# Layer 3 of a four-layer graph network: VectorE's second joined block and the preceding unit's reciprocals change places

## The chip, the cores and the metric

The program runs on one core of a Trainium2 chip, in one launch. The metric is the device time of a launch in microseconds (us). The core has five engines with queues of their own: TensorE (PE; its weight loads are listed apart as PEld), VectorE (DVE), ScalarE (ACT), GpSimd (POOL) and SyncE (SP), which here only issues DMA transfers. An engine works through its queue in the order in which the program was written, and waits where an input or a buffer is not there yet.

## The reference

`x` is 32 x 512 x 64 (32 batches, 512 nodes, 64 features) and `adj` a normalised 512 x 512 adjacency matrix. Four layers follow each other, each with a layer norm before it and a residual around it; layers 0 to 2 are a plain graph layer, a two-step propagation and a small attention. The change is in layer 3, graph attention with 8 heads of width 128 and an output layer of the same form:

```
def gat_layer(x, graph, W, b):
    h = x @ W
    s = jnp.einsum('bnd,bmd->bnm', h, h) * graph
    s = jnp.where(s == 0.0, NEG_INF, s)
    a = jax.nn.softmax(s, axis=2)
    return jnp.einsum('bnm,bmd->bnd', a, h) + b
heads = jax.vmap(lambda W, b: gat_layer(flow_x, graph, W, b))(Wh, bh)
...
x = jax.nn.leaky_relu(cat, negative_slope=0.01)
out = gat_layer(x, graph, W_out, b_out)
return jax.nn.leaky_relu(out, negative_slope=0.01)
```

## The kernel before

Everything is float32. Layers 0 to 2 run first (to about 460 us of the span); layer 3 takes the rest. It is cut into **units**: a unit is two attention maps of 512 x 512 that are worked on together (`k` = 0, 1), held as four row blocks `r` = 0 to 3 of 128 partitions x 1024 elements. For each two batches there are eight units of heads (`Heads`) and one of the output layer (`Out`), which comes some units later; 16 pairs of batches make 144 units.

A unit goes through these steps (line numbers are those of the profile):

- `scores(r)`, PE, L370: row block `r` of the scores into a PSUM tile of pool `ps_s`.
- `maxima(r)`, DVE, L382: masks the block, copies it negated to SBUF (`p_att`), and takes row maxima into `top`. Two instructions a block.
- `spread_out`, L389 and L392: DVE transposes the maxima (`top_t`), SP sends them to DRAM (`top_row`, four small transfers). `spread_in`, L398: SP reads them back, spread over all partitions (`topb`, 512 KB).
- `shift(r)`, POOL, L404: subtracts `topb` from block `r`.
- `exps(r)`, ACT, L413: the exponential. For `r` = 0 and 2 it stays in SBUF; for `r` = 1 and 3 it goes to a PSUM tile `e_ps` of the same pool `ps_s`.
- `join(r)`, DVE, L416, `r` = 1 and 3: adds the exponentials of blocks `r` - 1 and `r`. The result is the joined block, and `e_ps` comes free.
- `totals`, PE L434, ACT L439: column sums of joined blocks 1 and 3 with a matmul of ones. `totals_out`, L446: SP and ACT send them to a small tile `parts`, 8 to a partition.
- `recips`, DVE, L452 and L455: adds the two sums and takes reciprocals (`rec_flow`, 128 x 8). `recips_out`, SP, L459: to DRAM (`rec_row`). `recips_in`, SP, L466: back from there, spread over 64 partitions for each map (`recb`, two transfers of 128 KB).
- `values(j)`, PE, L422: the blocks times the features, into `av` (pool `ps_v`, one buffer). `normalize`, DVE, L472: `av` times `recb` gives `o_att` and frees `av`.
- `y_pe`, `y_act`, `y_dve` (L553, L563, L571): the head's product with its weights, bias and leaky ReLU. `back`, `back_dve`, `back_pool`, `store`: the end of an output unit.

`ps_s` has two buffers (line 1260), and they are taken in turn by blocks 2 and 3 of the scores, blocks 0 and 1 of the next unit's scores, and the two `e_ps`, all in one period. So block 2 of the next period's scores needs what `join(1)` frees, and block 3 what `join(3)` frees.

The order is written by hand. `planned` (L703) makes a function `period(t)` (L711), which is called for `t` = -10 onward and writes one period: the steps of units of different age next to each other. `unit(1)` is the unit one period old, `unit(2)` two periods, and so on; a step that a unit hasn't got does nothing. The schedule is kept as written for all five engines, so VectorE's queue in a period is: `maxima` 2 and 3 of the present unit, the transpose of `top`, `y_dve` of unit(4), `normalize` of unit(3), `maxima` 0 and 1 of the coming unit, `join(1)` of unit(1), `recips` of unit(2), `back_dve`, `join(3)` of unit(1), and now and then a small reduction (`features`, `judge_product`, or the difference in `make_v`). SP's queue is: `recb` of unit(3), `top_row`, `topb`, one `parts`, `rec_row`, and the stores of an output unit.

```
def join(self, r):
    nc.vector.tensor_tensor(self.p[r], self.joined, self.p[r - 1], OP.add)
...
def recips(self):
    self.rec = tiny.tile([P, 8], F32, name="rec_flow")
    nc.vector.tensor_reduce(
        self.rec, self.parts.rearrange("p e i -> p i e"), AX.X, OP.add
    )
    nc.vector.reciprocal(self.rec, self.rec)
...
def normalize(self):
    self.o = wk.tile([P, N], F32, name="o_att")
    nc.vector.tensor_tensor(self.o, self.av, self.recb, OP.mult)
```

Of the kernel before, what the change touches and what calls it, by code (L numbers as in the profile page):

```python
# [22 lines left out]
def fast_form(  # L23
# [645 lines left out]
    def any_zero():  # L669

        def across(src, rows, name):
            ps = ps_m.tile([P, P], F32, name=name, tag="m")
            n = src.shape[0]
            nc.tensor.transpose(ps[:rows, :n], src, ident[:n, :n])
            return ps[:rows, :n]

        own = tiny.tile([P, 1], F32, name="own")
        nc.vector.tensor_reduce(own, least, AX.X, OP.min)
        two = tiny.tile([1, 2], F32, name="two")
        nc.vector.tensor_reduce(two[:, 0:1], across(own, 1, "own_ps"), AX.X, OP.min)  # L680
        best = tiny.tile([B // 2, 2], F32, name="best")
        nc.vector.tensor_reduce(
            best,
            across(least_out, B // 2, "out_ps").rearrange("b (k f) -> b k f", k=2),
            AX.X, OP.max,
        )
        worst = tiny.tile([B // 2, 1], F32, name="worst")
        nc.vector.tensor_reduce(worst, best, AX.X, OP.min)
        nc.vector.tensor_reduce(
            two[:, 1:2], across(worst, 1, "worst_ps"), AX.X, OP.min  # L690
        )
        flag = tiny.tile([1, 1], F32, name="flag")
        nc.vector.tensor_reduce(flag, two, AX.X, OP.min)
        nc.vector.scalar_tensor_tensor(
            again, flag, 0.0, unsound, op0=OP.is_equal, op1=OP.max
        )
# [6 lines left out]
    def planned(units, products):  # L703

        class Nothing:
            def __getattr__(self, name):
                return lambda *args: None

        nothing = Nothing()

        def period(t):  # L711
            def unit(lag):
                return units[t - lag] if 0 <= t - lag < len(units) else nothing

            now, ahead = unit(0), unit(-1)
            for r in range(2, C):
                now.scores(r)
            unit(3).recips_in()
            unit(4).y_pe()
            unit(1).shift(0)  # L720
            unit(1).exps(0)
            unit(4).y_act()
            u, h = products.get(t - 1, (None, 0))
            if u and h == H - 1:
                u.keep_product()
            unit(1).shift(2)
            unit(1).exps(2)
            for r in range(2, C):
                now.maxima(r)
            now.spread_out()  # L730
            now.spread_in()
            for r in range(2):
                ahead.scores(r)
            unit(4).y_dve()
            unit(3).normalize()
            for r in range(2):
                ahead.maxima(r)
            unit(4).back()
            unit(2).totals()
            unit(2).totals_out()  # L740
            unit(1).shift(1)
            unit(1).exps(1)
            u, h = products.get(t, (None, 0))
            if u:
                u.product(h)
            for j in range(C):
                unit(2).values(j)
            unit(1).join(1)
            unit(1).shift(3)
            unit(1).exps(3)  # L750
            unit(5).back_pool()
            unit(-2).make_gs()
            unit(2).recips()
            unit(2).recips_out()
            unit(5).store()
            unit(4).back_dve()
            unit(1).join(3)
            unit(-3).features(3)
            unit(-2).judge_product()
            unit(1).make_v()  # L760
            unit(-4).make_hx()
            unit(-2).make_g()
            for step in range(3):
                for lag, odd in ((step - 7, 0), (step - 11, 1)):
                    u = unit(lag)
                    if getattr(u, "i", None) == 0 and u.b % 2 == odd:
                        u.features(step)
            if t == len(units):
                any_zero()

        return period
# [1067 lines left out]
```

## Time and profile before

| | |
|---|---|
| median of 3 runs | 2102.34 us (2097.67 to 2103.63) |
| profiled execution, time / span | 2099.58 us / 2097.8 us |
| mean granted TensorE clock | 0.985 |
| layer 3, first to last transpose of `top` (L389) | 460.7 to 2053.4 us, 144 of them |
| busy in that stretch of 1592.7 us: PE, DVE, POOL, ACT | 1542.6, 1404.6, 1379.1, 1029.0 us |

The stretch of 1592.7 us divided by its 143 periods gives 11.14 us for a period. Four engines are busy in it, none of them all the time: what one unit needs is spread over six periods, and the engines hand its parts to each other. So busy shares alone don't say what sets the period; the waits and the order within one period do. A row of a timeline gives the start, the duration, the engine, the line and operation, and in brackets how long the engine had been idle and what ended that.

### The profile page before, as it was taken

What the parts mean: (1) busy time and instruction counts of PE and PEld (TensorE: products, weight loads), DVE (VectorE), ACT (ScalarE), POOL (GpSimd) and SP (SyncE); (2) the same over time, 40 slices, a digit from 0 to 9 for tenths busy, and PEclk for the clock granted to TensorE, in tenths of its full rate; (3) what the DMA queues carried; (4) which work ended last, traced back from release to release, by engine and by line L of the source; (5) the groups of instructions that cost most, each with busy time, mean ns of one, the idle gap of its engine ahead of it and who ended that gap; (6) DMA issues with size and microseconds to landing.
All of it is one profiled execution on the core that took longest, in us unless ns stands there. A gap on an engine that the chain in (4) does not pass through costs nothing. (4 is left out here: it accounts for less than half of the span.)

```text
span 2097.8 us, 33009 instructions
## 1 busy us (share of the span) xinstructions
PE 2002.6 (95%) x11038; PEld 813.8 (39%) x11038; DVE 1786.2 (85%) x4257; ACT 1227.9 (59%) x1944; POOL 1432.7 (68%) x697
## 2 busy tenths in 40 slices
PE   7999999988999999999999999999999999999995
PEld 4667676652333333333333333333333333333321
DVE  6699997667998989898989898989888888988983
ACT  3444443335666666666666666666666666766553
POOL 3000000018898889888888988888888888888995
PEclk9999999989999999999999999999999999999998
DMA  5000000001222222222222222222222222222222
GB/s 139 1 1 2 1 2 1 1 22 57 77 75 69 78 77 73 78 76 82 68 78 77 72 77 77 77 71 74 68 77 73 77 67 73 77 71 74 77 68 78
DMA packets 135780, 129.35 MB, mean 62 GB/s; under 512 B 92792, under 2 KB 98080, under 8 KB 135472
## 3 DMA queue, kind: packets, MB, share of 16 engines
q1 hardware_dynamic: 116368, 126.35, 19.8%
q10 hardware_dynamic: 18720, 0.59, 0.5%
q8 instruction: 89, 1.46, 0.3%
q0 software_dynamic: 512, 0.20, 0.1%
q14 instruction: 91, 0.75, 0.1%
HBM read 119.48 MB, written 5.37 MB: 60 GB/s over the span
## 5 line engine op out<-in xcount | busy, mean ns | idle before, releaser
L404 POOL TENSOR_TENSOR p_att<-p_att,topb 128x1024 f32<-128x1024 f32 x576 | 1347.4, 2374 | 232.7 <-DMA topb<-top_row 130.6
L382 DVE CUSTOM_DVE_ANT_0 p_att<-s_ps,flow_neg 128x512 f32<-128x512 f32 x1152 | 727.8, 685 | 53.6 <-PE s_ps L370 51.9
L370 PE MATMUL s_ps<-hx,g 64*128 64x512 f32 x2048 | 545.3, 615 | 34.3 <-DVE p_att L416 24.6
L413 ACT ACTIVATE e_ps<-p_att 128x1024 f32<-128x1024 f32 x288 | 295.8, 1028 | 174.2 <-DVE top L382 107.8
L413 ACT ACTIVATE p_att<-p_att 128x1024 f32<-128x1024 f32 x288 | 304.2, 1056 | 149.6 <-POOL p_att L404 146.6
L416 DVE TENSOR_TENSOR p_att<-e_ps,p_att 128x1024 f32<-128x1024 f32 x288 | 346.5, 1203 | 24.7 <-ACT e_ps L413 24.4
L370 PEld LDWEIGHTS s_ps<-hx,g 64*128 64x128 f32 x2048 | 179.4, 186 | 343.1 <-DVE top L382 163.2
L422 PE MATMUL av<-p_att,hd 128*64 128x512 f32 x1024 | 264.3, 593 | 2.2 <-DVE o_att L472 2.0
L422 PE MATMUL av<-p_att,hn 128*64 128x512 f32 x1024 | 263.7, 592 | 0.0
L1053 POOL TENSOR_TENSOR x<-x,bias_b 128x512 f32<-128x512 f32 x16 | 20.3, 1271 | 280.0 <-DVE hn L826 280.0
L571 DVE SCALAR_TENSOR_TENSOR cat<-y_ps,bh,cat 128x512 f32<-128x512 f32 x256 | 178.1, 737 | 6.2 <-ACT cat L563 3.4
L563 ACT ACTIVATE cat<-y_ps,bh 128x512 f32<-128x512 f32 x256 | 161.7, 680 | 11.8 <-PE y_ps L553 8.7
L434 PE MATMUL tot_ps<-p_att,ones 128*32 128x512 f32 x1152 | 154.8, 610 | 1.6 <-DVE cat L571 0.5
L553 PE MATMUL y_ps<-o_att,wh_sb 64*128 64x512 f32 x512 | 143.2, 589 | 0.0
L598 PE MATMUL gT_ps<-cat,wo_sb 128*64 128x512 f32 x512 | 138.1, 618 | 0.0
L439 ACT COPY tot<-tot_ps 128x512 f32<-128x512 f32 x144 | 84.4, 586 | 85.0 <-PE tot_ps L434 83.6
L422 PEld LDWEIGHTS av<-p_att,hd 128*64 128x64 f32 x1024 | 73.2, 137 | 152.2 <-issue 141.2
L422 PEld LDWEIGHTS av<-p_att,hn 128*64 128x64 f32 x1024 | 74.8, 137 | 144.9 <-issue 144.9
L472 DVE TENSOR_TENSOR o_att<-av,recb 128x512 f32<-128x512 f32 x144 | 98.3, 683 | 34.9 <-DMA recb<-rec_row 34.6
L547 ACT COPY g<-g_ps 128x512 f32<-128x512 f32 x128 | 70.3, 588 | 95.3 <-PE g_ps L535 95.3
L977 PE MATMUL acc<-v,s 64*128 64x65 f32 x2048 | 124.1, 280 | 0.7 <-DVE s L963 0.4
L977 PEld LDWEIGHTS acc<-v,s 64*128 64x128 f32 x2048 | 121.2, 195 | 5.9 <-DVE o L993 1.2
(181 smaller groups left out, 2028.2 us busy)
## 6 DMA issues: line engine op xcount, KB each, us to landing
topb<-top_row SPq DMA_DIRECT2D x144, 512.0 KB
recb<-rec_row SPq DMA_DIRECT2D x288, 128.0 KB
top_row<-top_t SPq DMA_DIRECT2D x576, 1.0 KB
out_dram<-y SPq DMA_DIRECT2D x32, 128.0 KB
x<-in_x_dram SPq DMA_DIRECT2D x3, 1024.0 KB
parts<-tot ACTq DMA_DIRECT2D x144, 4.0 KB
parts<-tot SPq DMA_DIRECT2D x144, 4.0 KB
rec_row<-rec_flow SPq DMA_DIRECT2D x144, 4.0 KB
```

What stands on the lines that cost most here:

```text
L370: nc.tensor.matmul(ps[:, k], lhsT=g[halves(k), r * P : (r + 1) * P], rhs=x[halves(k), :], start=True, stop=True,)
L382: nc.vector.tensor_tensor_reduce(out=self.p[r][:, k], in0=ps[:, k], in1=flow_neg[:, r], scale=-1.0, scalar=BIG, op0=OP.add, op1=OP.min, ac ...
L404: nc.gpsimd.tensor_tensor(self.p[r], self.p[r], self.topb, OP.subtract)
L413: nc.scalar.activation(to, self.p[r], AF.Exp, scale=-1.0)
L416: nc.vector.tensor_tensor(self.p[r], self.joined, self.p[r - 1], OP.add)
L422: nc.tensor.matmul(self.av[halves(k), :], lhsT=self.v(k, j) if j % 2 else self.less_next(k, j), rhs=self.p[j][:, k], start=(j == 0), stop= ...
L434: nc.tensor.matmul(ps[q : q + 32, :], lhsT=ones, rhs=self.p[2 * e + 1][:, k], start=True, stop=True,)
L553: nc.tensor.matmul(ps, lhsT=wh_sb[halves(k), 2 * self.i + k, :], rhs=self.o[halves(k), :], start=True, stop=True,)
L563: nc.scalar.activation(self.cat[:, k], self.y[k], AF.Identity, bias=bh01[:, h : h + 1], scale=0.01)
L571: nc.vector.scalar_tensor_tensor(self.cat[:, k], self.y[k], bh[:, h : h + 1], self.cat[:, k], op0=OP.add, op1=OP.max,)
L598: nc.tensor.matmul(self.gps[halves(k), :], lhsT=wo_sb[:, h, :], rhs=Heads.cat.pop((self.b + k, h)), start=(h == 0), stop=(h == H - 1),)
L977: nc.tensor.matmul(self.acc[k][:, r], lhsT=self.s[b // 2][halves(k), b % 2, r * P : (r + 1) * P], rhs=self.v[halves(k), b], start=(b == 0) ...
```

## The change

One line of `period(t)` moves up by four: `join(3)` of unit(1) stands in front of `recips` of unit(2), no longer behind it and `back_dve`. No instruction is added or taken away, and no buffer or size is changed. VectorE's queue is then `join(1)`, `join(3)`, `recips`, `back_dve`; the queues of PE, ACT, POOL and SP hold the same instructions in the same order as before.

```
             unit(1).exps(3)
             unit(5).back_pool()
             unit(-2).make_gs()
+            unit(1).join(3)
             unit(2).recips()
             unit(2).recips_out()
             unit(5).store()
             unit(4).back_dve()
-            unit(1).join(3)
             unit(-3).features(3)
             unit(-2).judge_product()
             unit(1).make_v()
```

More of the change, by code (lines that the diff above doesn't have):

```diff
@@ L752, in period @@
             unit(-2).make_gs()
+            unit(1).join(3)
             unit(2).recips()
@@ L756, in period @@
             unit(4).back_dve()
-            unit(1).join(3)
             unit(-3).features(3)
```

## The prediction

> **What bounds the kernel now.** I read the page's busy times first, then VectorE's waits, then the timeline of single periods.
>
> ```profile
> PE 2002.6 (95%) x11038; PEld 813.8 (39%) x11038; DVE 1786.2 (85%) x4257; ACT 1227.9 (59%) x1944; POOL 1432.7 (68%) x697
> L416 DVE TENSOR_TENSOR p_att<-e_ps,p_att 128x1024 f32<-128x1024 f32 x288 | 346.5, 1203 | 24.7 <-ACT e_ps L413 24.4
> ```
>
> PE is the busiest; an instruction that is to move costs 1.2 us of VectorE. What VectorE waits for:
>
> ```profile
> DVE rec_flow L452 <- DMA parts<-tot: 77.1, 118, 2.4
> DVE p_att L382 <- PE s_ps L370: 51.9, 61, 2.2
> DVE o_att L472 <- DMA recb<-rec_row: 34.6, 34, 4.9
> ```
>
> Total us, times, longest. The first line is what the change goes for: in 118 of 144 periods VectorE stands in front of the reciprocals until `parts` lands, 0.65 us each time. The third will matter more. One period, cut from the timeline of all engines:
>
> ```profile
> 1213.85 0.21 DVE L389 STREAM_TRANSPOSE top_t<-top 128x32 f32<-128x32 f32 x1
> 1215.27 0.68 DVE L472 TENSOR_TENSOR o_att<-av,recb 128x512 f32<-128x512 f32 x1
> 1215.87 0.68 DVE L382 CUSTOM_DVE_ANT_0 p_att<-s_ps,flow_neg 128x512 f32<-128x512 f32 x1
> ...
> 1216.84 1.03 PE L422 MATMUL av<-p_att,hd 128*64 128x512 f32 x4
> ...
> 1218.35 1.23 DVE L416 TENSOR_TENSOR p_att<-e_ps,p_att 128x1024 f32<-128x1024 f32 x1
> ...
> 1218.69 1.03 ACT L413 ACTIVATE e_ps<-p_att 128x1024 f32<-128x1024 f32 x1 [0.38 <-POOL p_att L404]
> ...
> 1220.24 0.17 DVE L452 TENSOR_REDUCE rec_flow<-parts 128x8 f32<-128x16 f32 x1 [0.67 <-DMA parts<-tot]
> ...
> 1220.44 0.20 DVE L455 RECIPROCAL rec_flow<-rec_flow 128x8 f32<-128x8 f32 x1
> 1220.56 1.17 DVE L416 TENSOR_TENSOR p_att<-e_ps,p_att 128x1024 f32<-128x1024 f32 x1
> 1220.67 0.34 SPq L459 DMA_DIRECT2D rec_row<-rec_flow  x1
> 1220.95 1.99 PE L370 MATMUL s_ps<-gs 64*128 64x512 f32 x8
> ...
> 1222.09 1.12 SPq L466 DMA_DIRECT2D recb<-rec_row  x2
> 1222.13 0.69 DVE L382 CUSTOM_DVE_ANT_0 p_att<-s_ps,flow_neg 128x512 f32<-128x512 f32 x1
> ...
> 1224.70 0.21 DVE L389 STREAM_TRANSPOSE top_t<-top 128x32 f32<-128x32 f32 x1
> ```
>
> Count from the transpose at 1213.85, which begins a period here. `o_att` starts at 1.42, the first `join` at 4.50; ACT has filled the second `e_ps` at 5.87 (1218.69 + 1.03); `parts` lands at 6.39, the reciprocals end at 6.79, the second `join` runs from 6.71 to 7.88, the maxima of blocks 2 and 3 start at 8.28, and 2.57 later comes the next transpose: 10.85 us.
>
> What ends last at 8.28? I compared the rows of many periods. PE goes without a gap from the column sums over `av` to block 2 of the scores, and the maxima start 1.1 to 1.2 us after that block (1220.95 to 1222.13). Where PE makes features for a coming unit in between, the period is 10.85 us (rows at 1035.25, 1136.27) or 11.12 us (1024.13, 1147.12) to the hundredth, however late `parts` or the second `join` came within some tenths. So PE, not VectorE, closes these periods. Only the two of nine periods without such work could start their maxima at 7.69 (shortest period 10.26 us), and there the second `join` ends last, near 7.9: 10.46 us. The period of an output unit takes 12.63. By nines: 3 x 10.85 + 3 x 11.12 + 2 x 10.46 + 12.63 = 99.5 us, against 100.2 us measured (9 x 11.14).
>
> **What the Trainium skill says.** "PSUM — Partial Sum Buffer", section "Engine vs sequencer instructions": VectorE's queue is a strict FIFO. The trace agrees: the second `join` had its input at 5.87 and started at 6.71, behind reciprocals that waited for `parts`. After the change it is the reciprocals that stand behind. "DMA: Bandwidth & Descriptors", section "Latency and other measured facts": the write receipt of the target dominates a transfer's fixed cost, HBM is the slowest, and the wait grows with HBM load. Here the reciprocals' 4 KB to DRAM took 1.42 us from issue (1220.67) until SP could issue what reads them (1222.09), but 2.40 us in another period (864.37 to 866.77).
>
> **The change part by part.** VectorE's work stays 10.4 us or so a period.
>
> *Removed:* the pause before L452. The second `join` can start when the first ends and `e_ps` is full: near 5.75 to 5.9, not 6.7. It ends at about 7.0, and the reciprocals at 7.3; `parts` (6.4) is there by then. In the PE-closed periods this buys nothing. In the two others the maxima can start at 7.69: 0.2 us each, 0.4 per nine, 6 us over 16 nines. About ten periods in which `parts` came late (the longest wait is 2.4 us) stand to gain half a microsecond each, 4 us after what later waits take back.
>
> *Moved back:* the reciprocals, from 6.8 to 7.3, and with them all that hangs on them: `rec_row`, then `recb` on SP's queue, then `o_att`. This loop runs once a period and costs:
> - reciprocals' end to the issue of `recb`: over 144 periods 1.65 us on average; 1.45 in the typical one, near 2.4 in 26 of them.
> - issue of `recb` to the start of `o_att`, in the 34 periods where VectorE waited for it: 3.4 to 4.6, mean 3.7 (3.66 without the two slowest).
> - `o_att` to the end of the reciprocals: 0.60 + four maxima 2.48 + first `join` 1.23 + reciprocals 0.40 = 4.71 before, and 1.15 more with the second `join` in it: 5.86.
>
> Before: 5.3 + 4.7 = 10.0 us, a microsecond under the period, so `o_att` seldom waits. After: 5.3 + 5.86 = **11.2 us**, over the period of 11.1. The loop has no slack left.
>
> *Who waits for a late `o_att`.* `av` has one buffer, so PE's first `values` matmul needs it; on time it starts at 2.98, and a late one 0.84 after `o_att` starts:
>
> ```profile
> 866.77 1.11 SPq L466 DMA_DIRECT2D recb<-rec_row  x2
> ...
> 870.52 0.69 DVE L472 TENSOR_TENSOR o_att<-av,recb 128x512 f32<-128x512 f32 x1 [2.30 <-DMA recb<-rec_row]
> ...
> 871.36 1.08 PE L422 MATMUL av<-p_att,hd 128*64 128x512 f32 x4 [0.62 <-DVE o_att L472]
> ```
>
> That period, an output unit's, took 13.32 us, not 12.63. So an `o_att` later than 2.14 (1.80 in an output unit's period) pushes PE, and the period with it.
>
> *Sum over nine periods*, starting behind an output unit, with o the start of `o_att`, L the length: next o = o + 5.86 + 5.3 - L, at least 1.42; L = the PE-closed length plus what o exceeds 2.14 by. I take 5.65 once, for the period with the stores (both waits are longer there). o / L: 1.42/10.26, 2.67/11.65, 2.18/10.89, 2.45/11.16, 2.45/11.43, 2.18/10.89, 2.45/11.43, 2.18/10.53 (there the reciprocals end last: o + 5.86 + 2.49), 2.81/13.62. Sum 101.9 against 99.5: +2.4 per nine, **+38 us** over 16. With the latency at its least, 5.0 throughout, the same sum is 99.3: **-3 us**. The real latency is a mixture of much 5.05 and some 5.5 to 6.3, and where a slow one falls in a period of 11.12 or behind an output unit it costs less than the mean does. I take three quarters, +29, less the 4 us of late `parts`: **+25 us**.
>
> *SP's queue:* `recb` would be issued at about 9 to 10 of the period and `top_row` of the next maxima at 11.1. That is free, except behind a slow `rec_row`. A late `recb` also shares the DMA engines with `top_row`: where `o_att` started at 2.43, `topb` was issued at 2.9 instead of 2.57 after the transpose. POOL's chain (`topb` at 2.57, shifts from 6.4 to 15.8, exponentials to 16.9, so 5.8 in the next period) stays under the later `join`; bound 0 to 0.35 us a period, taken 0. The output unit's `back_dve` sits in a period where VectorE then waits for PE 1.5 us: nothing.
>
> The profiled execution took 2099.58 us: 2124.6. The runs' median lies 2.8 us above it, so I forecast **2127 us**.
>
> **The rivals.**
> - *Faster: the pause is filled and the loop holds.* One place: issue of `rec_row` to start of `o_att`. If that stays at 5.0 or the lateness is absorbed, then -3 us and up to -6 from late `parts`: 2093 us. For it: 104 of 144 periods have the short first leg, and 77.1 us of waits vanish from the engine. Against it: 40 have not. It decides below about 5.05.
> - *Nothing to measure:* both effects cancel, or `o_att` is late only where PE is late anyway: 2102 us. For it: PE closes seven of nine periods.
> - *Slower still:* late `recb` transfers push `top_row`, `topb` and POOL by 0.35 us in half of the periods, 25 us more: 2152 us. For it the 2.9 above; against it POOL's idle time before its shifts.
> - *The change doesn't act*, as ACT fills `e_ps` late: it was full at 5.7 to 6.9, so the second `join` can wait up to a microsecond in front of ready reciprocals. That lengthens the same loop and belongs to my forecast.
>
> **How the numbers follow.** Forecast 0.56 (2109 to 2147 by its latency of 5.1 to 5.5), slower still 0.10, nothing 0.14, faster 0.20. Slower 0.66, same 0.14, faster 0.20, where 0.3%, some 6 us, is what a measurement of this kernel can tell from no change. Range 2092 to 2154: it leaves out the deeper half of faster and of slower still.
>
> **What would show it.** Right: the wait of L452 for `parts` nearly gone from 77.1 us; that of `o_att` for `recb` up from 34.6 to about 100 us or more; PE's `av` waiting for `o_att` beyond its 21 times; periods of 11.12 stretched to about 11.4. Wrong: `o_att` still starting at 1.42 in most periods; or `join` 3 starting no earlier than 6.7; or POOL waiting longer for `topb`.

## The result, and the profile after

| | before | changed |
|---|---|---|
| median | 2101.34 us (4 runs, the three of the first table and one more) | 2123.07 us (2117.63 to 2124.75, 4 runs) |
| ratio to before | | 1.0101, 95% interval 1.0076 to 1.0125 |
| profiled execution, time / span | 2099.58 / 2097.8 us | 2124.75 / 2123.0 us |
| mean distance of two transposes of `top` | 11.14 us | 11.31 us |

The change costs 1.0%. Busy times and the moved instruction, from the page of the changed kernel:

```profile
PE 2009.9 (95%) x11038; PEld 818.1 (39%) x11038; DVE 1791.7 (84%) x4257; ACT 1227.6 (58%) x1944; POOL 1431.2 (67%) x697
L416 DVE TENSOR_TENSOR p_att<-e_ps,p_att 128x1024 f32<-128x1024 f32 x288 | 351.6, 1224 | 34.6 <-ACT e_ps L413 33.4
```

The same instructions run, and VectorE's busy time of 1786.2 us has become 1791.7. So of the 25 us by which this execution is longer, some 20 are waiting on VectorE. Its waits in the changed kernel (total us, times, longest):

```profile
DVE o_att L472 <- DMA recb<-rec_row: 97.7, 98, 4.9
DVE p_att L382 <- PE s_ps L370: 62.2, 82, 3.6
...
DVE rec_flow L452 <- DMA parts<-tot: 2.7, 4, 0.9
```

The pause in front of the reciprocals, 77.1 us before, is gone. In its place `o_att` waits for `recb`: 97.7 us, where it was 34.6. And PE waits for `o_att` with its first `values` matmul, 12.9 us together before (first) and 54.2 us now (second):

```profile
PEld av L422 <- DVE o_att L472: 9.2, 13, 2.1
PE av L422 <- DVE o_att L472: 3.7, 8, 1.0
```

```profile
PEld av L422 <- DVE o_att L472: 28.1, 35, 4.4
PE av L422 <- DVE o_att L472: 26.1, 30, 3.4
```

One late period, cut from the timeline of all engines of the changed kernel:

```profile
815.79 1.10 SPq L466 DMA_DIRECT2D recb<-rec_row  x2
...
817.50 0.21 DVE L389 STREAM_TRANSPOSE top_t<-top 128x32 f32<-128x32 f32 x1
...
820.74 0.69 DVE L472 TENSOR_TENSOR o_att<-av,recb 128x512 f32<-128x512 f32 x1 [1.74 <-DMA recb<-rec_row]
821.49 1.08 PE L422 MATMUL av<-p_att,hd 128*64 128x512 f32 x4 [0.84 <-DVE o_att L472]
...
823.81 2.45 DVE L416 TENSOR_TENSOR p_att<-e_ps,p_att 128x1024 f32<-128x1024 f32 x2
...
826.17 0.16 DVE L452 TENSOR_REDUCE rec_flow<-parts 128x8 f32<-128x16 f32 x1
826.36 0.20 DVE L455 RECIPROCAL rec_flow<-rec_flow 128x8 f32<-128x8 f32 x1
826.60 0.34 SPq L459 DMA_DIRECT2D rec_row<-rec_flow  x1
...
828.01 1.12 SPq L466 DMA_DIRECT2D recb<-rec_row  x2
...
829.40 0.21 DVE L389 STREAM_TRANSPOSE top_t<-top 128x32 f32<-128x32 f32 x1
```

This is the loop in full, in a period with an unusually slow `recb`. It is issued at 815.79, and `o_att` can start at 820.74: 4.95 us later, where the mean of the 98 waits is 3.65, and 3.24 after the transpose, where 1.42 is on time. Both joins follow each other without a gap (x2, 2.45 us), the reciprocals end at 826.56, 5.82 us after `o_att` started, and the next `recb` leaves at 828.01. PE's first `values` matmul starts 3.99 after the transpose and not at 2.98: the period takes 11.90 us, not 10.85.

That the start of `o_att` sets the length can be read over many periods. 46 periods of layer 3 have matmuls for the `g` of a coming unit in them and are otherwise alike. They take 11.12 to 11.15 us, most of them, where `o_att` starts early enough. In the changed kernel it starts later than 2.2 us after the transpose in 30 of them (3 before), and 19 of these last 9.02 us from that start, to within 0.05: 11.41 with a start at 2.39, 11.69 at 2.67, 12.02 at 3.00.

### The profile page after: what moved, and what is told of

Its sections match the earlier page's. It is cut to its first block, busy times and chain, and to the rows that moved or that the text cites. A ratio compares the mean times of both kernels' runs of the same rounds, so it can differ in the third digit from the quotient of the medians.

```text
span 2123.0 us, 33010 instructions
## 1 busy us (share of the span) xinstructions
PE 2009.9 (95%) x11038; PEld 818.1 (39%) x11038; DVE 1791.7 (84%) x4257; ACT 1227.6 (58%) x1944; POOL 1431.2 (67%) x697
## 5 line engine op out<-in xcount | busy, mean ns | idle before, releaser
L416 DVE TENSOR_TENSOR p_att<-e_ps,p_att 128x1024 f32<-128x1024 f32 x288 | 351.6, 1224 | 34.6 <-ACT e_ps L413 33.4
L472 DVE TENSOR_TENSOR o_att<-av,recb 128x512 f32<-128x512 f32 x144 | 99.3, 689 | 98.8 <-DMA recb<-rec_row 97.7
```

## The experiments

The medians of the kernel before differ by up to 0.4% between chips, so each ratio below is to runs of before on the same chip. Three theories of the loss are told apart. Theory 1 is the loop of the prediction. Theory 2 is that late `recb` transfers hinder `top_row` and `topb`, and so POOL. Theory 3 is that VectorE is held in front of the reciprocals by an `e_ps` that isn't full.

### Nobody waits for `recb`

```
-            nc.vector.tensor_tensor(self.o, self.av, self.recb, OP.mult)
+            nc.vector.tensor_tensor(self.o, self.av, urow, OP.mult)
```

The changed order with this edit:

> The changed order, but normalize multiplies by a constant row instead of recb, so the division by the sums is left out; the reciprocals, rec_row and recb are still made and moved at the same places, only nobody waits for recb. Theory 1 (the loop reciprocals - recb - o_att - first values matmul - join - reciprocals has no slack left): all of the loss goes, o_att starts at 1.4 after the transpose in nearly every period, and the time falls below the kernel before, to about 2083 us (2078 to 2092). Theory 2 (late recb transfers hinder top_row and topb, and POOL is late): these transfers stay as late, so the time stays at 2115 us or more. Theory 3 (VectorE is held in front of the reciprocals by a second e_ps that is not full): stays at 2115 or more as well.

The order before with it:

> The order before, with the same constant row in normalize, so the division by the sums is left out here too: the control for the run with the changed order. Theory 1: only the few waits for recb go (34.6 us of VectorE, 12.9 us of PE), so about 2090 us (2085 to 2097), some 5 to 10 us above the changed order without recb. Theories 2 and 3: about 2090 us too, but 20 us or more below the changed order without recb.

Measured: changed order 2088.07 us, ratio 0.9962 (0.9952 to 0.9973); order before 2087.11 us, ratio 0.9960 (0.9953 to 0.9968). The whole difference of 1% between the two orders is gone once nobody waits for `recb`. The transfers are still made late: the issue of `recb` lies 1.55 us ahead of the next transpose (median), in the changed kernel 1.59, in the kernel before 2.60. That excludes theory 2 as the cause. POOL's wait for `topb` says the same; it is no longer in the changed kernel (second) than before (first):

```profile
POOL p_att L404 <- DMA topb<-top_row: 130.6, 88, 3.4
```

```profile
POOL p_att L404 <- DMA topb<-top_row: 129.7, 78, 3.5
```

Theory 3 is excluded too: in the changed order without `recb`, VectorE waits longer for `e_ps` (94.9 us) than in the changed kernel (33.4 us), and yet nothing is lost.

One half of the expectation failed: the changed order is not 5 to 10 us faster than the other. Its waits, without `recb`, against those of the order before without `recb`:

```profile
DVE p_att L416 <- ACT e_ps L413: 94.9, 107, 7.3
DVE rec_flow L452 <- DMA parts<-tot: 7.4, 6, 4.8
```

```profile
DVE rec_flow L452 <- DMA parts<-tot: 79.5, 131, 3.8
DVE p_att L416 <- ACT e_ps L413: 43.0, 21, 6.7
```

In the changed order (first) VectorE waits for the second `e_ps` instead of for `parts` (second): 102 us against 122 together. The pause has mostly changed its name. By periods, counted in one trace of each: the 41 without extra work on PE gain 4.3 us in sum by the changed order, and those in which PE makes features for a coming unit (`g` or `hx`) lose 5.3. Filling the pause is worth nothing on the whole that these two runs could tell.

### Half of the join in front

```
+        def join_half(self, r, k):
+            nc.vector.tensor_tensor(
+                self.p[r][:, k], self.joined[:, k], self.p[r - 1][:, k], OP.add
+            )
...
+            unit(1).join_half(3, 0)
             unit(2).recips()
             unit(2).recips_out()
             unit(5).store()
             unit(4).back_dve()
-            unit(1).join(3)
+            unit(1).join_half(3, 1)
```

> The second join is cut into its two halves (one attention map each, 128 x 512); the first half goes in front of the reciprocals, the second stays behind them. Theory 1: the loop grows by 0.6 us only, to about 10.5 to 10.6, under the period of 11.1, and the pause before the reciprocals is filled: waits of o_att for recb 40 to 60 us, time 2090 to 2097 us, so a little faster than before. Theory 3 (it is the waiting for e_ps in front of the reciprocals that costs): the first half waits for the same e_ps, so most of the loss stays: 2112 us or more. If loss goes simply with the share that is moved: about 2112 us too.

The control has both halves behind `back_dve`:

> The second join cut into two halves, both behind the reciprocals: the control for the cut. All theories: within 4 us of before (2097 to 2105), since one more fixed cost of about 0.1 us a period falls on VectorE where PE closes most periods.

Measured: half in front 2092.81 us, ratio 0.9985 (0.9976 to 0.9994); both behind 2103.56 us, ratio 1.0038 (1.0027 to 1.0049), 8 us slower than its before, twice what was expected: a half takes 0.68 us (median), so two of them take 0.16 us more than one `join` of 1.2 us, not 0.1. Against this control, half in front gains 0.5%, where the whole join in front loses 1.0% against its own. Waits with half in front:

```profile
DVE o_att L477 <- DMA recb<-rec_row: 44.6, 48, 5.0
DVE p_att L419 <- ACT e_ps L413: 25.7, 56, 1.1
DVE rec_flow L457 <- DMA parts<-tot: 8.8, 14, 2.0
```

`o_att` waits 44.6 us for `recb`, as expected, and the pause for `parts` is down to 8.8 us. A share of 0.7 us fits into the loop's slack; 1.2 us doesn't. A cost that goes with the moved share, or with waiting for `e_ps` (25.7 us here at the halves), would have made this run slower than its control.

### One part alone: past `back_dve` only

```
             unit(2).recips()
             unit(2).recips_out()
+            unit(1).join(3)
             unit(5).store()
             unit(4).back_dve()
-            unit(1).join(3)
```

> One part of the change alone: the second join goes in front of back_dve and of the stores, but stays behind the reciprocals. Every theory: nothing, since only the periods of output units have a back_dve and VectorE waits for PE 1.5 us there: within 3 us of before, ratio 0.9985 to 1.0015. A larger difference would mean that the place behind back_dve is a part of the cost.

Measured: 2103.02 us, ratio 0.9996 (0.9986 to 1.0005). So the step past `back_dve` costs nothing, and what is left is the step past the reciprocals.

### Letting PE need `av` later

```
+            early_g = not isinstance(unit(4), Out)
+            if early_g:
+                unit(-2).make_g()
             for j in range(C):
                 unit(2).values(j)
...
+            if early_g:
+                unit(-2).keep_g()
             unit(1).make_v()
             unit(-4).make_hx()
-            unit(-2).make_g()
+            if not early_g:
+                unit(-2).make_g()
+                unit(-2).keep_g()
```

`keep_g` holds the copies that stood at the end of `make_g`.

> The changed order, and PE makes the coming units' g (0.86 us of matmuls, three periods of nine) in front of the values matmuls instead of behind them; the copies of g stay where they were on ScalarE. PE does the same work, but needs the av buffer 0.9 us later in those periods, so a late o_att is hidden there. If a late o_att costs its time by holding PE in front of the first values matmul (theory 1), a third to two thirds of the loss goes: 8 to 15 us under the changed kernel, ratio to before 1.003 to 1.007, and PE's waits of av for o_att fall from 54 us to under 35 us. If the late o_att costs its time on VectorE itself (the first join and the maxima behind it come later), nothing is gained: ratio 1.009 to 1.012.

> The order before with g in front of the values matmuls: the control for moving g. Theory 1: o_att is seldom late here (PE waits 12.9 us for it), so little to gain: 0 to 6 us faster than before, ratio 0.997 to 1.000.

> The half join in front of the reciprocals together with g in front of the values matmuls: a candidate for a better kernel than either. Theory 1: the remaining waits of PE for o_att (17 us with the half join) shrink to about 8: 3 to 10 us faster than the half join alone, ratio to before 0.994 to 0.998.

Measured, as ratios to before: changed order 1.0149 (1.0131 to 1.0167), order before 1.0051 (1.0035 to 1.0066), half 1.0003 (0.9994 to 1.0012). All three expectations were missed. The edit itself costs 0.5%: a period with `g`, 11.12 us before, takes 11.47 with `g` in front of the values. And over its control the changed order still loses 1.0149 / 1.0051 = 1.0097, all of it. By the expectation that would speak for a cost on VectorE itself; the single periods say otherwise. A period of the changed order with `g` first:

```profile
898.28 0.21 DVE L392 STREAM_TRANSPOSE top_t<-top 128x32 f32<-128x32 f32 x1
...
900.98 0.69 DVE L475 TENSOR_TENSOR o_att<-av,recb 128x512 f32<-128x512 f32 x1 [1.19 <-DMA recb<-rec_row]
...
901.37 1.13 PE L538 MATMUL g_ps<-hx,m 64*128 64x512 f32 x4
...
902.43 1.08 PE L425 MATMUL av<-p_att,hd 128*64 128x512 f32 x4
```

Here the edit did what it was to do: `o_att` starts 2.70 after the transpose, PE makes `g` meanwhile, and `av` starts at 4.15, as in periods with an early `o_att`; the period is 11.47 us to the hundredth. It isn't the only one: of 19 periods with `g` whose `o_att` starts between 2.5 and 3.22, 12 take 11.47 to 11.49 us. So VectorE can be this late without a cost of its own. But the loop went on just as late, and PE's waits for `o_att` at `av` are still 51.1 us:

```profile
PEld av L425 <- DVE o_att L475: 28.3, 28, 3.4
PE av L425 <- DVE o_att L475: 22.8, 28, 2.5
```

In one trace of each, the loss by the changed order in the 46 periods with `g` fell from 14.6 to 8.0 us in sum, while the 41 periods without extra work on PE, which gained 6.7 by it, now lose 0.8. Hiding a late `o_att` in one place doesn't shorten the loop. This fits theory 1, with the wait for `av` as the place where the time shows and the length of the loop as what decides it; but the run was to show less loss, and didn't.

### A loop of another length, the order unchanged

The next runs leave the order on every engine as it is and alter only how `recb` is brought. SP then issues one transfer for it and not two. First a single transfer for both maps:

```
-            for k in range(2):
-                nc.sync.dma_start(
-                    self.recb[halves(k), :], self.rec_row[k : k + 1, :].to_broadcast([F, N])
-                )
+            nc.sync.dma_start(
+                self.recb,
+                self.rec_row.rearrange("k (o n) -> k o n", o=1).to_broadcast([2, F, N]),
+            )
```

> The changed order, and recips_in brings recb with one transfer of 256 KB for both maps instead of two of 128 KB issued one behind the other (the two issues take 1.10 us now, one is expected at about 0.5). The loop gets shorter outside VectorE by about 0.5 us, from 11.1 to 10.6, while the order on every engine stays that of the change. Theory 1 (the length of the loop is what costs): nearly all of the loss goes, ratio to before 0.994 to 1.001, waits of o_att for recb under 60 us. If what costs is the second join in front of the reciprocals in itself, through VectorE's or PE's order and not the way through DRAM: ratio stays at 1.007 or more.

> The order before with the single recb transfer: the control. Its loop (10.0 us) has slack already, so only some of the 34.6 us of waits for recb go: ratio to before 0.995 to 0.9995. Theory 1 puts the changed order with the single transfer within 0.4% of this one; otherwise they stay 0.8% or more apart.

> Half of the second join in front of the reciprocals and the single recb transfer: the candidate for a version that beats both kernels. The waits for recb nearly go as in the run without recb (0.996), and the shortest periods are 10.26 us: ratio to before 0.994 to 0.998.

Measured against 2102.61 us for before: changed order 2642.36 us, ratio 1.2565 (1.2548 to 1.2582); order before 2509.17 us, 1.1936 (1.1915 to 1.1958); half in front 2567.21 us, 1.2205 (1.2184 to 1.2227). The transfer didn't get shorter, it got far longer. From the timeline of the order before with it:

```profile
1215.04 0.53 SPq L465 DMA_DIRECT2D recb<-rec_row  x1
1217.26 0.21 DVE L389 STREAM_TRANSPOSE top_t<-top 128x32 f32<-128x32 f32 x1
...
1222.08 0.69 DVE L472 TENSOR_TENSOR o_att<-av,recb 128x512 f32<-128x512 f32 x1 [4.61 <-DMA recb<-rec_row]
1222.92 1.97 PE L422 MATMUL av<-p_att,hd 128*64 128x512 f32 x4 [2.50 <-DVE o_att L472]
```

The issue takes 0.53 us as expected, but `o_att` follows 7.0 us after it, and 7.6 on average where VectorE waits, not 3.7. (The `values` matmuls behind this wait took 1.97 us and not 1.08, and the mean granted clock of the run was 0.948, where before it was 0.985.) The test missed its aim and became one in the other direction: the loop is now so long that it sets nearly every period. `o_att` waits for `recb` in 135 of the 144 periods of the order before, 137 with half in front and 141 of the changed order:

```profile
DVE o_att L472 <- DMA recb<-rec_row: 421.0, 135, 9.0
```

```profile
DVE o_att L477 <- DMA recb<-rec_row: 450.6, 137, 9.2
```

```profile
DVE o_att L472 <- DMA recb<-rec_row: 514.0, 141, 9.0
```

So each piece of `join` in the loop must be paid in nearly each period. Over 144 periods, half a join in front costs (2567.21 - 2509.17) / 144 = 0.40 us, a whole one (2642.36 - 2509.17) / 144 = 0.93 us; from `o_att` to the end of the reciprocals they add 0.58 and 1.09 us on average in the traces. The difference lies in another piece of the loop: from the reciprocals to the issue of `recb` it takes 1.70 us on average in the order before, but 1.54 and 1.57 with the half and the whole join in front. Why that piece is shorter is open. The cost goes with the share here, where in the kernel with its own `recb` the first half was free. That fits theory 1.

Then a transfer that spreads over all partitions like that of `topb`:

```
-            for k in range(2):
-                nc.sync.dma_start(
-                    self.recb[halves(k), :], self.rec_row[k : k + 1, :].to_broadcast([F, N])
-                )
+            nc.sync.dma_start(self.recb, self.rec_row[0:1, :].to_broadcast([P, N]))
```

> The changed order, and recips_in is one transfer over all 128 partitions of the first map's row, so both maps are divided by the first map's sums (the second map's reciprocals are left out of the division). The two 128 KB transfers become one of 256 KB that is spread like topb's. The issue should take 0.35 to 0.55 us instead of 1.10, so the loop shrinks from 11.1 to about 10.5 us with the order on every engine as in the change. Theory 1 (the loop's length costs): most of the loss goes, ratio to before 0.996 to 1.002, waits of o_att for recb 30 to 65 us. If the order on VectorE or PE costs in itself: ratio 1.007 or more, waits near 98 us.

Measured: 2100.49 us, ratio 0.9992 (0.9982 to 1.0002). Its wait of `o_att`:

```profile
DVE o_att L469 <- DMA recb<-rec_row: 58.8, 55, 5.3
```

The issue is down to 0.32 us, and from it to `o_att` it takes 3.39 us on average where VectorE waits, against 3.65 in the changed kernel. A quarter of a microsecond less on the way of `recb`, with the order of the change untouched, and the loss of 1.0% is gone. The order before wasn't run with this transfer, so a part of the gain may come to it as well; but with no wait for `recb` at all that order gains 0.4%, so at least some 0.6 of the 1.0% is the loop. `topb` is also issued 0.2 us earlier here (mean), which the runs without `recb` show to be no part of the cost. The loop stands at the edge of the period: that is theory 1, from the side on which the order can't be blamed.

## Why the prediction was right

- *What is removed:* the pause before L452 went from 77.1 to 2.7 us, and the joins follow each other, as said. Of the 41 periods without extra work on PE, 18 now take the 10.26 us that were forecast, where 2 did before.
- *What it is worth:* the sum gave 10 us for this (6 for those periods, 4 for late `parts`). Those periods did gain 6.7 us in sum. But the runs without `recb` show no difference between the orders on the whole: the other periods lose as much. This is the term that was over-priced: behind `parts` stood `e_ps`, filled at nearly the same time. It counted little against the +38.
- *The loop:* expected 5.3 from the reciprocals to `o_att` plus 5.86 back to the reciprocals. Measured in the changed kernel: 1.58 + 3.65 = 5.2 (means, the second of the periods in which VectorE waited), and 5.82 in the median period. The sum, 11.05, leaves nearly no slack in a period of 11.14. Why `rec_row` is slow in some periods, and whether the load of HBM has to do with it, no run here shows. The run with the shorter way has 1.59 + 3.39 = 5.0, and came out at -0.08% of before (-0.18 to +0.02); the working for a latency of 5.0 had given -3 us, -0.14%, which lies within that.
- *Who waits:* `o_att` later than 2.14 after the transpose pushes PE. It started later than that (or than 1.80 with an output unit) in 66 of 140 periods that could be read in the trace, by 33 us in sum; before, in 10, by 3 us. The waits forecast at "about 100 us or more" came to 97.7; PE's wait at `av` grew as said; the periods with `g`, 11.12 before, have a median of 11.41; those of seven output units went to 13.1 to 13.4 us. An eighth took 16.68, with a `recb` that VectorE waited 3.97 us for.
- *The sum over nine periods* was multiplied by 16, but the kernel doesn't run 16 such nines. Its list of units puts 8 of the output units between those of heads and the other 8 behind all heads, so only 7 nines of this shape follow each other. They grew by 2.0 us each (700.3 to 714.5 in sum, the one slow period included), where the sum gave 2.4. The 50 periods after them, heads alone, grew by 6.4 us, for which no sum was made. So the loop was right and the cost of one nine about right, but the way from there to the total was not.
- *The three quarters* taken of the +38 were a choice, not a measurement, and so was the zero for POOL. The second is borne out by the runs without `recb`. With the first the forecast came to 2127 us, 4 us above the median; since the 16 nines and the 4 us of late `parts` were both wrong, coming this close took some luck.
- *The rivals:* "faster" needed the latency at 5.0; it was 5.2, and with 5.0 made by hand the time is that of before. "Slower still" by way of `topb` is excluded by the runs without `recb`. "Nothing to measure" is excluded by the interval of the ratio. That the change acts was plain from the first line of waits.

## What to carry to other kernels

A wait that an engine stands in may be the cheapest place to stand: look at what the instruction behind the wait starts, and add up the whole way until that comes back to the same engine. If this loop, with what is to be put in front, is longer than the period, the filled pause comes back elsewhere, later and dearer. Put into the pause only as much as the loop has slack (here half a join was free and a whole one was not), or shorten the loop first; hiding its lateness at one of its stops only moves the bill to the next.

## What the runs showed of the hardware

- A transfer of 256 KB written as 2 x 64 partitions took 7.6 us from issue to use, the same bytes as two transfers of 64 partitions 3.7, and as one over 128 partitions 3.4 (means of the periods in which VectorE waited for it). The Trainium skill, "DMA: Bandwidth & Descriptors", section "Why a DMA increments its semaphore by 16 and not by 1", says that the number of DMA engines is the largest up to 16 that divides the slowest dimension of both access patterns: for a pattern that begins with 2 that would be two engines. The trace agrees: from the first to the last of the 128 packets of 2 KB that carry this transfer, 2.0 are under way on average, against 7.4 in the changed kernel and 7.1 with one transfer over 128 partitions.
- Moving 0.86 us of PE work, matmuls of form 64 x 128, between others of form 128 x 64 lengthened the period by 0.35 us with no more work. The Trainium skill, "TensorEngine Tiling (Array Packing)", section "Key Properties", says that changing the tiling mode drains TensorE; the trace agrees in that the starts are 1.01 and 1.06 us apart at the two borders of `g`, and 0.86 between `values` of one form. That a drain is what takes this time isn't shown.
